# One written order per pass, with named PSUM tiles, for the three Fourier layers of a token-fusion kernel

## The chip, the cores and the metric
The kernel runs on one core of a Trainium2 chip. The metric is the device time of one execution in microseconds (us), lower is better; a profile of one execution gives the instructions of each engine with their times.

## The reference, cut to what matters
64 images of 256x256 go through a Fourier neural operator of four layers with 32 channels, then through one attention and feed-forward block together with 77 text rows. Per layer:
```python
x_ft = jnp.fft.rfft2(v)                        # only 24 x 12 modes are kept
out1 = jnp.einsum('bixy,ioxy->boxy', x_ft[:, :, :M1, :M2], W1)
out2 = jnp.einsum('bixy,ioxy->boxy', x_ft[:, :, -M1:, :M2], W2)
x1 = jnp.fft.irfft2(out_ft, s=(Sx, Sy))        # out_ft: zeros, with out1 and out2 set
x2 = jnp.einsum('bcxy,cd->bdxy', v, w_w[i]) + w_b[i][None, :, None, None]
v = x1 + x2
v = (v - mean) * jax.lax.rsqrt(var + BN_EPS)   # mean, var over batch, x, y
v = v * bn_g[i][None, :, None, None] + bn_b[i][None, :, None, None]
if i < L - 1:
    v = jax.nn.relu(v)
```

## The kernel before
The images lie in HBM as `v`, 1 MB for each of the 8 chunks of a batch element. Each of layers 0, 1 and 2 is one call of `layer(i, ...)`, which makes one pass per batch element `b` (64 passes). It turns the mixed modes of `mix_d[i]` into the layer's activated image, stores it, and at once takes the forward transforms of that image and the sums of squares for the next layer. The statements run under `tc.manual_schedule()`, so each engine executes its instructions in the order in which they are written. SP issues all loads and stores of the layer, in written order too.

The steps of a pass, with their lines:
- `load_am` (L574), `scale_am` (L594, on POOL): the modes of one batch element are loaded into a buffer `am` and multiplied by the batch-norm scale (spread out in `sk`) into one of two tiles `ams`.
- `spread` (L605, L609): the inverse transform along x. Two groups of matmuls fill PSUM, and VectorE (DVE) transposes each in 32x32 blocks, straight from PSUM, into `y_`.
- `pre(b, t)`, once for each chunk: inverse transform along y (L624) and, from layer 1 on, the 1x1 convolution of the loaded chunk `vin` (L635), into two PSUM tiles; relu into `vo`, one half by ScalarE (ACT, L642), one by DVE (L643); the store of `vo` (L644); a block transpose of `vo` into `t32` on DVE (L647). `load_v` (L588) then loads the chunk four ahead. In layer 0 there is no `vin`; the input rows come with `load_x`.
- `product(b, t)`: `vo` times the next layer's weights (L659), and on ACT the square with a running sum (L666), whose result goes back to PSUM.
- `along_y(b)`: the forward transform along y, 128 matmuls in a row over all of `t32` (L676), then two block transposes out of PSUM into `zt` on DVE (L686).
- `along_x(b)`: the forward transform along x (L699), an ACT copy (L706) and a store (L707).

All PSUM tiles come from one pool `lp` of four buffers, each two banks, named `ring` in the profile, taken in turn. `vo` comes from a pool `lo` of four buffers, `vin` from `li` of four, `t32` from `lt` of five. The order of a pass is that of two loops at the end of `layer`: for each chunk, `pre` of it and `product` of the one before; after chunk 1 `along_y`, and after chunk 3 `along_x`, of the batch element before; after chunk 5 `spread` of the next.

Of the kernel before, what the change touches and what calls it, by code (L numbers as in the profile page):

```python
# [16 lines left out]
S = 256  # L17
C = 32
# [107 lines left out]


# [8 lines left out]
def tile_fno_fusion_transformer(ctx: ExitStack, tc: tile.TileContext, a, cst_d, grid_d, out):  # L136
# [371 lines left out]
    def layer(i, st, src, dst, acc):  # L508
# [7 lines left out]
        with ExitStack() as cx:  # L516
            def pool(name, bufs, **kw):
# [3 lines left out]
            op, yp, ap_, cp, xp, zp, tp = (  # L521
                pool(n, k, reuse_waits="tile")
                for n, k in (("lo", 4), ("ly", 2), ("la", 2), ("lc", 1), ("lx", 2), ("lz", 1), ("lt", 5))
            )
            pp = pool("lp", 4, space=PSUM)
# [29 lines left out]
            sk = cp.tile([128, 16, 32], F32, name="sk")  # L555
            for _, p0, cs in halves:
                nc.vector.tensor_copy(
                    sk[p0:p0 + 64],
                    s_[p0:p0 + 64, cs].rearrange("p (c o) -> p c o", o=1).to_broadcast([64, 16, 32]),
                )  # L560
# [8 lines left out]
            am, y_, t32, vin, vo = {}, {}, {}, {}, {}  # L569

            def load_am(b):
                am[b] = ap_.tile([128, 16 * C], F32, name="am")
                for n in range(2):
                    nc.sync.dma_start(  # L574
                        am[b][64 * n:64 * n + 2 * KX],
                        mix_d[i][b].rearrange("p k c -> (p k) c")[:, 512 * n:512 * n + 512],
                    )
# [12 lines left out]
            def scale_am(b):  # L590
                a_ = am.pop(b)
                for n in range(2):
                    hv = slice(64 * n, 64 * n + 2 * KX)
                    nc.gpsimd.tensor_tensor(  # L594
                        ams[b % 2][hv], a_[hv], sk[hv].rearrange("p c k -> p (c k)"), ALU.mult
                    )

            def spread(b):

                y_[b] = yp.tile([128, 2, 32, C], F32, name="y_")  # L600
                for h in range(2):
                    ps = pp.tile([128, 2, 512], F32, name="ring")
                    for n in range(2):
                        hv = slice(64 * n, 64 * n + rows_)
                        nc.tensor.matmul(  # L605
                            ps[:, n, :], lhsT=EX[hv, 128 * h:128 * h + 128], rhs=ams[b % 2][hv],
                            start=True, stop=True, skip_group_check=True,
                        )
                    nc.vector.transpose(  # L609
                        y_[b][:, h].rearrange("p q c -> p c q"),  # L610
                        ps.rearrange("p n (c k) -> p (n c) k", k=32),
                    )

            def four():

                t2 = [pp.tile([128, 2, 512], F32, name="ring") for _ in range(2)]
                return t2, [t2[n // 2][:, n % 2] for n in range(4)]

            def pre(b, t):
                t2, ps = four()  # L620
# [9 lines left out]
                if i:  # L630
                    v = vin.pop((b, t))
                    for k in range(4):
                        for n in range(4):
                            j = (n + k) % 4
                            nc.tensor.matmul(  # L635
                                ps[n][32 * j:32 * j + 32], lhsT=ws[32 * n:32 * n + 32],
                                rhs=v[32 * n:32 * n + 32, 2 * j:2 * j + 2, :], start=False, stop=True,
                                skip_group_check=True, tile_position=(32 * n, 32 * j),
                            )
                o = vo[b, t] = op.tile([128, 8, S], F32, name="vo")  # L640
                of = o.rearrange("p (n r) y -> p n (r y)", r=2)
                nc.scalar.activation(of[:, 0:2], t2[0], AF.Relu)  # L642
                nc.vector.tensor_scalar(of[:, 2:4], t2[1], 0.0, None, ALU.max)  # L643
                nc.sync.dma_start(dst[b][:, t], o)  # L644
                if t % 2 == 0:
                    t32[b, t // 2] = tp.tile([128, 8, 16, C], F32, name="t32")
                nc.vector.transpose(  # L647
                    t32[b, t // 2][:, :, 8 * (t % 2):8 * (t % 2) + 8, :].rearrange("p y s c -> p s y c"),
                    o.rearrange("p s (y l) -> p s y l", l=32),
                )  # L650

            def product(b, t):

                o = vo.pop((b, t))
                t2, ps = four()
# [8 lines left out]
                for n in range(2):  # L664
                    at = 2 * (8 * b + t) + n
                    nc.scalar.activation(t2[n], t2[n], AF.Square, accum_out=acc[:, at:at + 1])  # L666

            zts = {}

            def along_y(b):  # L670
                t2, ps = four()
                for k in range(8):
# [9 lines left out]
                for j in range(4):  # L682
                    t32.pop((b, j))
                zt = zts[b] = zp.tile([128, 2, 32, C], F32, name="zt")
                for h in range(2):
                    nc.vector.transpose(  # L686
                        zt[:, h].rearrange("p k c -> p c k"),
                        t2[h].rearrange("p n (s c) -> p c (n s)", c=C),
                    )

            def along_x(b):
                zt = zts.pop(b)
                ps = pp.tile([128, 2, 512], F32, name="ring")
                for g in range(3):
                    n = 0
                    for h in range(2):
                        for r in range(2):
                            k0 = M * r + 4 * g
                            nc.tensor.matmul(  # L699
                                ps[:, 0, 96 * g:96 * g + 96],  # L700
                                lhsT=zt[:, h, k0:k0 + 4, :].rearrange("p k c -> p (k c)"),
                                rhs=FX[:, h, 48 * r:48 * r + 96], start=n == 0, stop=n == 3,
                            )
                            n += 1
# [4 lines left out]
            load_am(0)  # L709
# [5 lines left out]
            scale_am(0)  # L715
            spread(0)
            for b in range(B + 1):
                for t in range(8):
                    if b < B:
                        pre(b, t)  # L720
                        nb, nt = (b, t + 4) if t < 4 else (b + 1, t - 4)
                        if i and nb < B:
                            load_v(nb, nt)
                    pb, pt = (b, t - 1) if t else (b - 1, 7)
                    if pb >= 0 and (b < B or t == 0):
                        product(pb, pt)
                    if b and t == 1:
                        along_y(b - 1)
                    if b and t == 3:
                        along_x(b - 1)  # L730
                    if b + 1 < B:
                        if t == 0:
                            load_am(b + 1)
                            if i == 0:
                                load_x(b + 1)
                        if t == 2:
                            scale_am(b + 1)
                        if t == 5:
                            spread(b + 1)
# [408 lines left out]
```

## Time and profile before

| what | value |
|---|---|
| median of 3 runs (lowest, highest) | 12364.16 us (12347.56, 12374.95) |
| the profiled execution, its own time | 12360.58 us |
| its span in the profile | 12358.8 us, 405064 instructions |
| busy in the span: PE, PEld | 11164.5 us (90%), 5874.0 us (48%) |
| busy in the span: DVE, ACT, POOL | 8774.8 us (71%), 6094.5 us (49%), 1412.7 us (11%) |
| DMA | 3485.06 MB, mean 282 GB/s |
| relu of half a chunk: ACT L642, DVE L643 | 1021 ns, 1209 ns |
| transpose of a chunk, DVE L647 | 2311 ns |
| square of half a chunk, ACT L666 | 1012 ns, and 190 ns to read the sum |
| transpose out of PSUM, DVE L686 | 1925 ns |

PE is TensorE's matmul, PEld its weight load, which overlaps with matmuls; matmuls are pipelined, so their durations overlap too. A line such as "L643 DVE TENSOR_SCALAR vo<-ring" names the source line, the engine, the operation, and the tile written and read. In a timeline the first two numbers are the start and the duration in us; brackets give the idle time of the engine before it and what ended it, "issue" where the profile shows nothing that it waited for. SPq is SP's queue of DMA issues; the short times there are those of issuing, not of moving the data.

### The profile page before, as it was taken

What the parts mean: (1) busy time and instruction counts of PE and PEld (TensorE: products, weight loads), DVE (VectorE), ACT (ScalarE), POOL (GpSimd) and SP (SyncE); (2) the same over time, 40 slices, a digit from 0 to 9 for tenths busy, and PEclk for the clock granted to TensorE, in tenths of its full rate; (3) what the DMA queues carried; (4) which work ended last, traced back from release to release, by engine and by line L of the source; (5) the groups of instructions that cost most, each with busy time, mean ns of one, the idle gap of its engine ahead of it and who ended that gap; (6) DMA issues with size and microseconds to landing.
All of it is one profiled execution on the core that took longest, in us unless ns stands there. A gap on an engine that the chain in (4) does not pass through costs nothing. (4 is left out here: it accounts for less than half of the span.)

```text
span 12358.8 us, 405064 instructions
## 1 busy us (share of the span) xinstructions
PE 11164.5 (90%) x182038; PEld 5874.0 (48%) x182038; DVE 8774.8 (71%) x10667; ACT 6094.5 (49%) x10249; POOL 1412.7 (11%) x1987
## 2 busy tenths in 40 slices
PE   6999999998799999999979999999999699999999
PEld 3444444443444444444434444444444366666666
DVE  6777777777776777777766777767777566666665
ACT  5555555555555555555544555555555333333333
POOL 0000000000000000000010000000000133333333
PEclk8999999999899999999989999999999799999999
DMA  7555555555899999888889989889899755555554
GB/s 226 200 199 203 203 201 201 201 200 210 325 354 349 349 351 350 348 347 348 346 302 352 354 346 355 339 339 353 346 351 352 247 234 227 219 228 233 218 223 152
DMA packets 589283, 3485.06 MB, mean 282 GB/s; under 512 B 95000, under 2 KB 144536, under 8 KB 188568
## 3 DMA queue, kind: packets, MB, share of 16 engines
q1 hardware_dynamic: 539520, 3392.84, 71.2%
q0 software_dynamic: 40880, 62.59, 2.0%
q8 instruction: 1423, 23.31, 0.8%
q10 hardware_dynamic: 7144, 3.72, 0.1%
q14 instruction: 316, 2.59, 0.1%
HBM read 1761.87 MB, written 1696.92 MB: 280 GB/s over the span
## 5 line engine op out<-in xcount | busy, mean ns | idle before, releaser
L666 ACT ACTIVATE ring<-ring 128x1024 f32<-128x1024 f32 x3072 | 3108.8, 1012 | 1186.4 <-PE ring L659 1148.7
L647 DVE STREAM_TRANSPOSE t<-vo 128x2048 f32<-128x2048 f32 x1536 | 3550.0, 2311 | 175.1 <-ACT vo L642 14.5
L659 PE MATMUL ring<-vo,w 32*32 32x512 f32 x49152 | 2849.3, 622 | 392.2 <-DVE zt L686 138.7
L642 ACT ACTIVATE vo<-ring 128x1024 f32<-128x1024 f32 x1536 | 1568.2, 1021 | 2997.7 <-PE ring L635 2378.9
L643 DVE TENSOR_SCALAR vo<-ring 128x1024 f32<-128x1024 f32 x1536 | 1857.7, 1209 | 608.2 <-PE ring L635 420.4
L676 PE MATMUL ring<-t,cst 32*32 32x512 f32 x49152 | 1864.7, 601 | 303.7 <-issue 302.1
L686 DVE STREAM_TRANSPOSE zt<-ring 128x1024 f32<-128x1024 f32 x384 | 711.8, 1925 | 1658.6 <-PE ring L676 1658.6
L659 PEld LDWEIGHTS ring<-vo,w 32*32 32x32 f32 x49152 | 761.3, 105 | 1898.7 <-ACT ring L666 477.0
L676 PEld LDWEIGHTS ring<-t,cst 32*32 32x32 f32 x49152 | 975.9, 103 | 1157.0 <-issue 707.8
L594 POOL TENSOR_TENSOR ams<-am,sk 48x512 f32<-48x512 f32 x384 | 486.9, 1268 | 8642.4 <-DMA am<-mix 8039.9
L635 PE MATMUL ring<-vin,ws 32*32 32x512 f32 x32768 | 1238.0, 606 | 22.1 <-issue 19.8
L699 PEld LDWEIGHTS ring<-cst,zt 128*128 128x128 f32 x4608 | 536.4, 194 | 174.6 <-ACT vo L642 161.6
L666 ACT ACTIVATION_READ_ACCUMULATOR ring<-ring 128x1 f32 x3072 | 584.1, 190 | 0.0
L1097 POOL DMA_DIRECT2D out_dram<-o x1024 | 504.4, 501 | 659.8 <-DVE o L1092 628.2
L699 PE MATMUL ring<-cst,zt 128*128 128x96 f32 x4608 | 568.7, 281 | 8.1 <-DVE zt L686 8.1
L896 PE MATMUL hp<-ch,win 128*32 128x512 f32 x4096 | 472.0, 601 | 8.3 <-DMA ch<-v 8.1
L635 PEld LDWEIGHTS ring<-vin,ws 32*32 32x32 f32 x32768 | 253.5, 103 | 407.9 <-issue 377.8
L605 PE MATMUL ring<-ams,cst 49*128 49x512 f32 (+1 forms) x1536 | 391.5, 621 | 37.6 <-POOL ams L594 27.2
L901 ACT ACTIVATE h<-hp,hbias 128x512 f32<-128x512 f32 x64 | 44.0, 687 | 595.5 <-PE hp L896 595.5
L419 PE MATMUL mps<-wm,xh 32*64 32x128 f32 (+1 forms) x4608 | 121.3, 374 | 203.4 <-ACT e L431 74.1
L1059 PE MATMUL pp<-zs,w 128*128 128x165 f32 x2048 | 302.1, 305 | 0.0
L1070 PE MATMUL pp<-g,w 128*128 128x165 f32 x2048 | 298.6, 303 | 0.0
(936 smaller groups left out, 11812.8 us busy)
## 6 DMA issues: line engine op xcount, KB each, us to landing
v<-vo SPq DMA_DIRECT2D x1536, 1024.0 KB
vin<-v SPq DMA_DIRECT2D x1024, 1024.0 KB
ch<-v SPq DMA_DIRECT2D x512, 1024.0 KB
mix<-ob SPq DMA_DIRECT2D x96, 512.0 KB
am<-mix SPq DMA_DIRECT2D x384, 96.0 KB
xin<-in_x_dram SPq DMA_DIRECT2D x16, 1024.0 KB
mv<-in_x_dram SPq DMA_DIRECT2D x256, 64.0 KB
out_dram<-o POOLq DMA_DIRECT2D x1024, 16.0 KB, 3.0
```

The source lines that it names most:

```text
L594: nc.gpsimd.tensor_tensor(ams[b % 2][hv], a_[hv], sk[hv].rearrange("p c k -> p (c k)"), ALU.mult)
L635: nc.tensor.matmul(ps[n][32 * j:32 * j + 32], lhsT=ws[32 * n:32 * n + 32], rhs=v[32 * n:32 * n + 32, 2 * j:2 * j + 2, :], start=False, sto ...
L642: nc.scalar.activation(of[:, 0:2], t2[0], AF.Relu)
L643: nc.vector.tensor_scalar(of[:, 2:4], t2[1], 0.0, None, ALU.max)
L647: nc.vector.transpose(t32[b, t // 2][:, :, 8 * (t % 2):8 * (t % 2) + 8, :].rearrange("p y s c -> p s y c"), o.rearrange("p s (y l) -> p s ...
L659: nc.tensor.matmul(ps[n][32 * j:32 * j + 32], lhsT=w4[i + 1][32 * n:32 * n + 32], rhs=o[32 * n:32 * n + 32, 2 * j:2 * j + 2, :], start=Tru ...
L666: nc.scalar.activation(t2[n], t2[n], AF.Square, accum_out=acc[:, at:at + 1])
L676: nc.tensor.matmul(ps[n][32 * j:32 * j + 32], lhsT=FYT[32 * n:32 * n + 32, k, :], rhs=t32[b, j][32 * n:32 * n + 32, k].rearrange("p s c -> ...
L686: nc.vector.transpose(zt[:, h].rearrange("p k c -> p c k"), t2[h].rearrange("p n (s c) -> p c (n s)", c=C),)
L699: nc.tensor.matmul(ps[:, 0, 96 * g:96 * g + 96], lhsT=zt[:, h, k0:k0 + 4, :].rearrange("p k c -> p (k c)"), rhs=FX[:, h, 48 * r:48 * r + 9 ...
L896: nc.tensor.matmul(hp[32 * g:32 * g + 32], lhsT=win[:, 7 - t:39 - t], rhs=ch[:, g], start=False, stop=t == 7, skip_group_check=True,)
L1097: nc.gpsimd.dma_start(out[b, 64 * n + 16 * g:64 * n + 16 * g + 16].rearrange("(p t) d -> p t d", t=2), o[32 * g + 8 * n:32 * g + 8 * n + 8 ...
```

## The change
The loops at the end of `layer` are replaced by a list of named steps, one list for layer 0 (`_FIRST`) and one for layers 1 and 2 (`_LATER`). Each entry is a step, a mark for the batch element that it works on (`'` one before the pass's, `''` two before, `^` one after), and its arguments, divided by points. The steps are the old ones, taken apart:
- `F(b, t, slots, by)` is the matmuls of `pre`, followed by `load_v`; `D` its relu and store, with a letter for each half, `a` for ACT and otherwise DVE; `T` the transpose of the chunk.
- `U(b, t, slots)` is the matmuls of `product`, `S` its two squares (all on ACT in both lists).
- `Z(b, k0, 2, slots)` is a quarter of `along_y`; `W(b, h, by)` takes one half out of PSUM: `v` as before by a transpose, `a` by an ACT copy into SBUF (`zs0`, `zs1`), from which `w` transposes later.
- `X` is `along_x`. `Y(b, h, slot, by)` and `y` are one half of `spread`, with the same two ways.

PSUM is four named tiles, ringA to ringD, and each entry says which it takes. `load_am` loads straight into `ams`, two batch elements ahead, and `scale_am` multiplies in place; `am` and `sk` are gone. `load_x` is issued at the start of a pass. The pool `lo` has five buffers in layer 0 and four later. The loop runs two passes more than there are batch elements, where before it ran one more.

```diff
+_FIRST = """
+    S'6.aa T'7 S'5.aa F0.CA.ad D0 U'7.BD w''1 S'7.aa U'2.CA S'2.aa F1.DB.aa T0 D1 F4.AC.da Y^0.D.a T'2 D4
+    Y^1.B.a U1.AD S1.aa X''C T'3 T'5 U0.BD Z'0.2.AC S0.aa F3.DB.da Z'2.2.AC D3 U3.BD S3.aa Z'4.2.AC y^1 T1
+    U4.DB Z'6.2.AC T4 S4.aa y^0 W'1.a W'0.v F5.DB.ad D5 F6.AD.ad F7.BC.ad D6 D7 F2.AD.ad U6.CB D2 U5.AD T6
+""".split()
+_LATER = """
+    Y^0.D.a w''1 U'7.CA S'7.aa T'1 F0.BD.aa D0 Y^1.C.a F1.AB.da U'6.CD D1 U0.AB S'6.aa S0.aa X''C T'7
+    F2.CB.da U'5.DA D2 F3.CB.da S'5.aa Z'0.2.AD Z'2.2.AD D3 U2.BC S2.aa y^0 Z'4.2.AD U3.CB T2 Z'6.2.AD y^1
+    S3.aa W'1.a F5.DC.aa W'0.v D5 F4.BA.aa T3 D4 T0 F7.CD.ad D7 U1.AB T4 S1.aa U4.DC S4.aa T5 F6.BA.da D6 T6
+""".split()
...
-            op, yp, ap_, cp, xp, zp, tp = (
+            op, yp, cp, xp, zp, tp = (
                 pool(n, k, reuse_waits="tile")
-                for n, k in (("lo", 4), ("ly", 2), ("la", 2), ("lc", 1), ("lx", 2), ("lz", 1), ("lt", 5))
-            )
-            pp = pool("lp", 4, space=PSUM)
+                for n, k in (("lo", 5 if i == 0 else 4), ("ly", 2), ("lc", 1), ("lx", 2), ("lz", 1), ("lt", 5))
+            )
+            pp = pool("lp", 1, space=PSUM)
...
+            def slot(n):
+                return pp.tile([128, 2, 512], F32, name=f"ring{n}")
...
             def load_am(b):
-                am[b] = ap_.tile([128, 16 * C], F32, name="am")
                 for n in range(2):
                     nc.sync.dma_start(
-                        am[b][64 * n:64 * n + 2 * KX],
+                        ams[b % 2][64 * n:64 * n + 2 * KX],
...
             def scale_am(b):
-                a_ = am.pop(b)
+                for _, p0, cs in halves:
+                    v = ams[b % 2][p0:p0 + 2 * KX].rearrange("p (c k) -> p c k", k=32)
+                    s = s_[p0:p0 + 2 * KX, cs].rearrange("p (c o) -> p c o", o=1)
+                    nc.gpsimd.tensor_tensor(v, v, s.to_broadcast([2 * KX, 16, 32]), ALU.mult)
...
+            def D(b, t):
+                t2, by = fs.pop((b, t))
                 o = vo[b, t] = op.tile([128, 8, S], F32, name="vo")
                 of = o.rearrange("p (n r) y -> p n (r y)", r=2)
-                nc.scalar.activation(of[:, 0:2], t2[0], AF.Relu)
-                nc.vector.tensor_scalar(of[:, 2:4], t2[1], 0.0, None, ALU.max)
+                for n in range(2):
+                    if by[n] == "a":
+                        nc.scalar.activation(of[:, 2 * n:2 * n + 2], t2[n], AF.Relu)
+                    else:
+                        nc.vector.tensor_scalar(of[:, 2 * n:2 * n + 2], t2[n], 0.0, None, ALU.max)
                 nc.sync.dma_start(dst[b][:, t], o)
...
+            def W(b, h, by):
+                ps = zs[b][0][h].rearrange("p n k -> p (n k)")
+                if by == "a":
+                    ev["z", b, h] = zp.tile([128, 1024], F32, name=f"zs{h}")
+                    nc.scalar.copy(ev["z", b, h], ps)
+                else:
+                    ev["z", b, h] = ps
+                    w(b, h)
...
-            for b in range(B + 1):
-                for t in range(8):
-                    if b < B:
-                        pre(b, t)
...
-                    if b and t == 1:
-                        along_y(b - 1)
-                    if b and t == 3:
-                        along_x(b - 1)
...
-                        if t == 5:
-                            spread(b + 1)
...
+            for b in range(B + 2):
+                if i == 0 and b + 1 < B:
+                    load_x(b + 1)
+                if b + 2 < B:
+                    load_am(b + 2)
+                    scale_am(b + 2)
+                for f, at, args in order:
+                    if 0 <= b + at < B and (b or f is not Y or at):
+                        f(b + at, *args)
```

## The prediction
> **What bounds the kernel now.** I read the stages first, then one pass of each kind of layer in the order of time, then the DMA share inside it. The three stretches below are layers 0, 1 and 2 (first `spread` to last `along_x`); columns are the stretch, its length, busy time of PE, PEld, DVE, ACT, POOL, the granted clock, DMA share, GB/s.
> ```profile
> 189.00:3071.00 2882.00, 2614.17 (x43010) 1217.22 (x43010) 2222.41 (x1286) 1602.51 (x2625) 168.44 (x139) 0.95 0.54 201
> 3175.00:6371.00 3196.00, 2918.05 (x59680) 1385.73 (x59676) 2271.16 (x1297) 1646.01 (x2637) 181.06 (x164) 0.99 0.90 347
> 6445.00:9608.00 3163.00, 2913.03 (x59369) 1379.81 (x59338) 2258.99 (x1280) 1636.35 (x2624) 164.81 (x137) 0.99 0.90 347
> ```
> They are 9241 of 12358.8 us. PE's busy time overlaps itself; no compute engine is full. Layers 1 and 2 differ from layer 0 in the DMA column: 0.90 against 0.54.
>
> Layer 0, one pass (timeline):
> ```profile
> 2026.45 2.31 DVE L647 STREAM_TRANSPOSE t<-vo 128x2048 f32<-128x2048 f32 x1
> 2028.69 1.19 DVE L643 TENSOR_SCALAR vo<-ring 128x1024 f32<-128x1024 f32 x1
> 2029.98 2.31 DVE L647 STREAM_TRANSPOSE t<-vo 128x2048 f32<-128x2048 f32 x1
> ...
> 2029.98 8.81 PE L676 MATMUL ring<-t,cst 32*32 32x512 f32 x256
> ...
> 2038.79 3.67 DVE L686 STREAM_TRANSPOSE zt<-ring 128x1024 f32<-128x1024 f32 x2 [6.50 <-PE ring L676]
> 2039.89 1.02 ACT L642 ACTIVATE vo<-ring 128x1024 f32<-128x1024 f32 x1 [7.37 <-PE ring L624]
> 2040.77 0.14 PEld L659 LDWEIGHTS ring<-vo,w 32*32 32x32 f32 x4 [1.32 <-DVE zt L686]
> ```
> See two regimes. In the chunk loop DVE has no pause: 1.29 + 2.24 = 3.53 us a chunk. Then `along_y` holds PE for 8.8 us while DVE (6.50) and ACT (7.37) wait, and afterwards PE waits for DVE's two block transposes out of PSUM. A transpose of `t` at 2008.24 recurs at 2052.51: a pass takes 44.27 us.
>
> Layer 1, the end of a pass in four stretches, columns as above:
> ```profile
> 4650.00:4654.00 4.00, 4.00 (x100) 2.22 (x89) 0.00 (x0) 0.00 (x0) 1.26 (x1) 0.68 0.99 403
> 4654.00:4658.00 4.00, 4.00 (x75) 1.46 (x52) 3.32 (x2) 0.76 (x1) 1.28 (x2) 1.00 0.21 82
> 4658.00:4660.00 2.00, 1.58 (x37) 0.67 (x40) 1.90 (x3) 0.48 (x2) 0.00 (x0) 1.00 0.00 0
> 4660.00:4664.00 4.00, 4.00 (x88) 2.06 (x81) 3.81 (x3) 3.64 (x6) 0.00 (x0) 1.00 0.93 299
> ```
> The same pass in the timeline of SP's queue and POOL:
> ```profile
> 4639.48 1.92 SPq L574 DMA_DIRECT2D am<-mix  x2
> 4642.57 0.43 SPq L588 DMA_DIRECT2D vin<-v  x1
> ...
> 4652.74 2.62 POOL L594 TENSOR_TENSOR ams<-am,sk 48x512 f32<-48x512 f32 x2 [45.59 <-DMA am<-mix]
> ...
> 4659.54 0.32 SPq L644 DMA_DIRECT2D v<-vo  x1
> ```
> The 96 KB `am` loads, issued at 4639.5 to 4641.4, are usable only at 4652.7: they stood behind the stores and loads before them. DMA runs without a break until about 4654.6, is idle about 5 us because nothing was issued between 4643.0 and 4659.5, and restarts. 258 chunks in 1600 us give 6.20 us a chunk, 49.6 us a pass; 0.894 of that (SP's queue 88.5% and instructions 0.9%) is 44.3 us of DMA work. So in these layers a better compute order can't beat 44 us.
>
> [...] here a 16 KB `out_dram` store lands after 3.0 us, which I use. [...]
>
> **The change part by part.**
> 1. PE's work per pass is the same: 8 F (`pre`), 8 U (`product`), `along_y` in four pieces Z, X, Y. Zero.
> 2. ACT gets three 128x1024 copies out of PSUM (two Y, one W; 1.0 us by the row of L642), and relu halves move: 9 on ACT and 7 on DVE in layer 0, 11 and 5 later, where it was 8 and 8. ACT per pass: 16 squares x 1.03 (start to start) + 9 x 1.0 + 3.3 = 28.8 us; later 30.8. Below any bound: no cost by itself.
> 3. Three of four y/z transposes now read SBUF. Not shown before: between 1.2 us (half of `t`) and 1.9 (strided, as now); I take 1.75, the present start to start, since the strided result stays. DVE in layer 0: 8 x 2.24 + 7 x 1.24 + 4 x 1.75 = 33.6 us (31.9 with the low value).
> 4. POOL multiplies in place with a broadcast operand in place of `sk`; `am` is loaded two batches ahead, so its 1.27 us pieces have a whole pass to hide in. `load_x` leads by a pass. Their SP entries move ahead of the pass's stores, and wait on readers that are done. Zero; if wrong, at most one 1.3 us piece a pass.
> 5. Order. I walked one pass by hand with times of the trace: F to its relu 1.18 us (layer 0) or 2.3 (later, two groups), U to its square 1.35, a square frees its slot after 1.1 and the second after 2.15, a relu after 1.05 (ACT) or 1.25 (DVE), a two-k piece of Z 1.8, X 2.9, Y 1.0.
> **Layer 0**: ACT's squares S'6, S'5 end at 4.2; F0, D0 5.65; S'7 and S'2 9.85; D1, both Y copies and D4's half 15.1; S1 17.25; U0, S0 21.05; F3, D3 23.5; U3, S3 27.5; U4, S4 31.1; F5, D5 33.4; F6, F7, F2 follow at 33.5, 34.6, 36.0; D2 38.4; the next S'6 38.6. DVE is busy 33.6 of it. Against 44.27: -5.8 us x 64 = **-371 us**. Bounds: DVE full, 34.5 (-625); three late hand-offs of 1.2 us, 42 (-145). The fifth `vo` buffer keeps stores away: DMA needs 0.54 x 44.27 = 24 us.
> **Layers 1 and 2**: the slots alone give about 43.8 us, PE's own work under 40. But `vo` keeps 4 buffers, and U and T of chunks are put off, so a buffer is held longer. The instruction order shows D6 waiting for the store of chunk 4, two chunks back, and the next pass's D1 for the store of chunk 6, 6.7 us after it is issued. Before, D waited for the store four chunks back (14.8 us). Now count DMA from the load after F5, where the queue starts empty: load, S5, load, S4, load, S7, load, S6, eight transfers of 1 MB at 403 GB/s = 2.6 us, and 3.0 us fixed: store 6 lands at **23.8**. D1 starts there; queued behind it on ACT are S'6 and S0, on DVE T'7 and D2, and PE's U0 waits for its slots. From D1 to the next F5's end: S'6 frees X's slot 2.15, X and its copy 5.9, F2, D2 9.6, F3, D3 13.3, Z'0 and Z'2 15.3, U2, S2 18.9, U3, S3 22.3, W' copy 23.4, F5 **25.5**. Sum 49.3 us, against 49.6: -0.3 x 128 = **-38 us**. What is late next is the DMA restart: idle 5 us a pass, as now. Bounds: 44.5 (store wait absent) and 52 (below).
> 6. Fill: one more partial pass per layer, setup of `sk` gone: within 30 us, taken as 0.
>
> Sum against the profiled execution (12360.6 us, 1.8 outside its 12358.8 us span): -409, 11952; the median of the runs is 3.6 above that execution, so **11955**.
>
> **Rivals.**
> - *The store wait doesn't bind* (transfers land sooner, or D1's chain is shorter than my walk). Then slots and DMA bind near 45.5: -371 - 4.1 x 128 = -896, 11468. For: the slot walk is 43.8, the DMA work 44.3. Against: the 13 us queue seen by `am`.
> - *Slower: PE starves in layers 1 and 2.* PE's weight loads of L676 waited 314.7 us for "issue" in layer 1, 4.9 a pass, while DMA was full, and the clock fell to 0.68 at 4650. If such gaps come on top of the D1 chain, with PE cold after the waits for stores, 53.2 us a pass: +3.6 x 128 - 371 = +90, 12454. It decides from 49.6 + 371/128 = 52.5 us a pass. Against: Z is cut in pieces, so instruction bursts are shorter.
> - *The order isn't what runs.* The layers stand under a manual schedule and the built queues follow the list; otherwise about 12364.
>
> **How the numbers follow.** Main case (48 to 51 us later) 0.55, its own range 11750 to 12200; no store wait 0.30; slower 0.11; nothing changed 0.04. A measurement of this kernel tells 0.2%, 25 us, from no change. Faster 0.85, same 0.04, slower 0.11. The range 11380 to 12340 leaves out the best end of the second case and most of the third.
>
> **What would show it.** Right: layer 0 about 2510 us with DVE near 0.87 and no DVE wait of 6 us on Z; in layers 1 and 2 about 49 us a pass, ACT and DVE at D1 and D6 (and the PE behind them) waiting for DMA of `v<-vo`, DMA idle before F5. Wrong: DMA share of 0.95 or more there (second case), or "issue" waits above 6 us a pass (third). A layer 0 above 42 us a pass breaks the first step.

## The result, and the profile after

The changed kernel takes 13397.85 us (median of 4 runs, 13390.38 to 13414.53) where the kernel before took 12369.56 beside it: ratio 1.0836, 95% interval 1.0816 to 1.0855. It is slower by 8.4%; the forecast was 11955 with a range up to 12340. The profiled execution took 13390.38 us, its span is 13388.6.

The stretches of layers 0, 1 and 2 (length, busy time of PE, PEld, DVE, ACT, POOL, granted clock, DMA share, GB/s):
```profile
197.00:3063.00 2866.00, 2305.78 (x42998) 1256.65 (x42998) 2134.85 (x1217) 1839.79 (x2878) 135.48 (x136) 0.91 0.56 202
3162.00:6843.00 3681.00, 3001.84 (x59394) 1358.04 (x59394) 2006.83 (x1092) 1976.57 (x3006) 138.95 (x139) 0.91 0.80 299
6945.00:10637.00 3692.00, 3006.51 (x59394) 1355.10 (x59394) 2007.36 (x1093) 1976.58 (x3006) 138.97 (x139) 0.91 0.79 299
```
Layer 0 is nearly as long as before (2866 us against 2882), where a gain of 371 us was forecast. Layers 1 and 2 are each some 500 us longer, and their DMA share fell from 0.90 to 0.80. Share times length is about the same as before (2945 and 2876 us in layer 1), so the extra time is pauses of DMA. The clock fell from 0.99 to 0.91.

Waits in the middle of layer 1 (4000 to 6000 us, 35 passes; total, times, longest):
```profile
PEld ringA L690 <- ACT vo L670: 208.7, 71, 6.4
ACT vo L670 <- DMA v<-vo: 193.8, 37, 6.7
DVE vo L672 <- DMA v<-vo: 178.5, 35, 6.3
DVE vo L672 <- PE ringD L690: 173.3, 35, 7.3
```
L670 and L672 are the relu halves of D on ACT and DVE, L654 and L643 the matmuls of F, L690 those of U, L701 the squares S, L716 Z, L678 T, L632 the transposes of y, L735 those of the y transform. Once a pass both relu engines wait some 5 us for a store, and PE waits behind ACT; once a pass (35 times) they also wait for a U. The places, in the timelines of ACT and of DVE:
```profile
5039.28 1.02 ACT L670 ACTIVATE vo<-ringA 128x1024 f32<-128x1024 f32 x1 [4.92 <-DMA v<-vo]
...
5047.14 1.02 ACT L670 ACTIVATE vo<-ringB 128x1024 f32<-128x1024 f32 x1 [2.45 <-PE ringD L654]
...
5051.76 1.02 ACT L670 ACTIVATE vo<-ringB 128x1024 f32<-128x1024 f32 x1 [1.78 <-PE ringD L690]
```
```profile
5039.30 1.23 DVE L672 TENSOR_SCALAR vo<-ringB 128x1024 f32<-128x1024 f32 x1 [4.59 <-DMA v<-vo]
5040.63 2.31 DVE L678 STREAM_TRANSPOSE t<-vo 128x2048 f32<-128x2048 f32 x1
5042.86 2.02 DVE L735 STREAM_TRANSPOSE zt<-zs 128x1024 f32<-128x1024 f32 x1
5044.75 2.31 DVE L678 STREAM_TRANSPOSE t<-vo 128x2048 f32<-128x2048 f32 x1
```
The first line of each is D6, waiting for the store of chunk 4. The second ACT line is D0 of the next batch element: it starts as DVE's fourth operation, T'1, ends. The third is D1. It takes the buffer of chunk 6, and what it waits for is not that chunk's store but U'6 (L690), the last step on PE that reads it: in the passes between 4000 and 6000 us D1 starts 0.07 us (median) after the last matmul of U'6. Stretches of this pass, columns as above:
```profile
5016.00:5019.00 3.00, 1.27 (x44) 0.65 (x46) 0.00 (x0) 0.00 (x0) 0.00 (x0) 1.00 0.14 52
5019.00:5022.00 3.00, 2.17 (x55) 0.93 (x51) 0.85 (x1) 2.90 (x5) 0.00 (x0) 1.00 0.00 0
...
5037.00:5040.00 3.00, 0.00 (x0) 0.00 (x0) 0.70 (x1) 0.72 (x1) 0.00 (x0) 0.68 1.02 431
5040.00:5043.00 3.00, 2.65 (x36) 0.91 (x40) 2.90 (x3) 1.66 (x3) 0.00 (x0) 0.50 1.00 423
```
DMA is idle ahead of F5's load (5024.70), then full; while it is full, D6 waits, PE stands still, and after that its clock is 0.50.

Layer 0, DVE's timeline at the end of the y transform:
```profile
2000.11 2.31 DVE L678 STREAM_TRANSPOSE t<-vo 128x2048 f32<-128x2048 f32 x1 [3.67 <-PE ringC L716]
2002.35 1.87 DVE L632 STREAM_TRANSPOSE y__19803<-zs 128x1024 f32<-128x1024 f32 x1
2004.06 1.86 DVE L735 STREAM_TRANSPOSE zt<-ringA 128x1024 f32<-128x1024 f32 x1
2005.77 1.20 DVE L672 TENSOR_SCALAR vo<-ringB 128x1024 f32<-128x1024 f32 x1
```
T4 waits until Z'6 has read `t32`, and y^0 and W'0 stand behind it. F6 needs the slot that W'0 empties.

**Where the 1030 us went**, from the stores of `xo` in SP's queue, one for each batch element: the 63 intervals from the first to the last in each layer, and the rest. The last interval or two of a layer are short, since little is left to do there (18.9 us for the last one in layer 0 after the change); the median interval of layer 0 is 44.3 us, and was 44.6.

| part | predicted, us | measured, us |
|---|---|---|
| layer 0, 63 passes (44.65 to 43.86 us each) | -371 | -50 |
| layers 1 and 2, 126 passes (49.1 to 56.35) | -38 | +910 |
| fill, drain and the way between layers | 0 | +170 |
| sum | -409 | +1030 |

### The profile page after: what moved, and what is told of

Its sections match the earlier page's. It is cut to its first block, busy times and chain, and to the rows that moved or that the text cites. A ratio compares the mean times of both kernels' runs of the same rounds, so it can differ in the third digit from the quotient of the medians.

```text
span 13388.6 us, 404421 instructions
## 1 busy us (share of the span) xinstructions
PE 11039.6 (82%) x182038; PEld 5864.0 (44%) x182038; DVE 8176.2 (61%) x10213; ACT 7012.8 (52%) x11267; POOL 1326.4 (10%) x1987
## 3 DMA queue, kind: packets, MB, share of 16 engines
q8 instruction: 1425, 23.35, 0.7%
## 5 line engine op out<-in xcount | busy, mean ns | idle before, releaser
L678 DVE STREAM_TRANSPOSE t<-vo 128x2048 f32<-128x2048 f32 x1536 | 3480.8, 2290 | 253.5 <-PE ringC L716 221.3
L716 PE MATMUL ringA<-t,cst 32*32 32x512 f32 x24576 | 2082.5, 603 | 72.2 <-issue 66.8
L690 PE MATMUL ringA<-vo,w 32*32 32x512 f32 x11264 | 989.7, 688 | 707.4 <-ACT vo L670 526.5
L716 PE MATMUL ringD<-t,cst 32*32 32x512 f32 x16384 | 1416.1, 606 | 76.8 <-issue 76.2
L670 ACT ACTIVATE vo<-ringB 128x1024 f32<-128x1024 f32 x832 | 851.3, 1023 | 1152.5 <-PE ringB L654 379.6
L690 PE MATMUL ringC<-vo,w 32*32 32x512 f32 x12288 | 1377.3, 673 | 65.2 <-issue 31.3
L701 ACT ACTIVATE ringB<-ringB 128x1024 f32<-128x1024 f32 x832 | 842.0, 1012 | 966.0 <-PE ringC L690 533.7
L690 PE MATMUL ringB<-vo,w 32*32 32x512 f32 x13312 | 1261.9, 635 | 38.1 <-issue 31.8
L716 PEld LDWEIGHTS ringA<-t,cst 32*32 32x32 f32 x24576 | 804.0, 103 | 641.8 <-issue 414.9
L701 ACT ACTIVATE ringC<-ringC 128x1024 f32<-128x1024 f32 x768 | 777.3, 1012 | 548.0 <-PE ringB L690 319.5
L690 PE MATMUL ringD<-vo,w 32*32 32x512 f32 x12288 | 992.3, 636 | 45.9 <-DVE vo L672 33.1
L654 PE MATMUL ringB<-vin,ws 32*32 32x512 f32 x12288 | 980.5, 675 | 0.0
L672 DVE TENSOR_SCALAR vo<-ringC 128x1024 f32<-128x1024 f32 x320 | 392.0, 1225 | 938.0 <-PE ringB L654 913.8
L670 ACT ACTIVATE vo<-ringA 128x1024 f32<-128x1024 f32 x384 | 392.3, 1022 | 1049.1 <-DMA v<-vo 674.3
L735 DVE STREAM_TRANSPOSE zt<-ringA 128x1024 f32<-128x1024 f32 x192 | 366.2, 1907 | 869.3 <-PE ringA L716 555.7
L701 ACT ACTIVATE ringD<-ringD 128x1024 f32<-128x1024 f32 x768 | 778.9, 1014 | 99.9 <-PE ringB L690 88.4
L672 DVE TENSOR_SCALAR vo<-ringD 128x1024 f32<-128x1024 f32 x320 | 391.5, 1223 | 657.1 <-PE ringB L643 320.5
L672 DVE TENSOR_SCALAR vo<-ringA 128x1024 f32<-128x1024 f32 x256 | 313.5, 1225 | 707.0 <-PE ringD L690 644.0
L690 PEld LDWEIGHTS ringA<-vo,w 32*32 32x32 f32 x11264 | 230.2, 110 | 1152.2 <-ACT vo L670 784.9
L701 ACT ACTIVATE ringA<-ringA 128x1024 f32<-128x1024 f32 x704 | 714.9, 1016 | 24.0 <-PE ringB L690 5.3
L672 DVE TENSOR_SCALAR vo<-ringB 128x1024 f32<-128x1024 f32 x192 | 233.4, 1216 | 640.5 <-DMA v<-vo 637.4
```

The lines of the kernel that those rows point to most:

```text
L654: nc.tensor.matmul(ps[n][32 * j:32 * j + 32], lhsT=ws[32 * n:32 * n + 32], rhs=v[32 * n:32 * n + 32, 2 * j:2 * j + 2, :], start=False, sto ...
L670: nc.scalar.activation(of[:, 2 * n:2 * n + 2], t2[n], AF.Relu)
L672: nc.vector.tensor_scalar(of[:, 2 * n:2 * n + 2], t2[n], 0.0, None, ALU.max)
L678: nc.vector.transpose(t32[b, t // 2][:, :, 8 * (t % 2):8 * (t % 2) + 8, :].rearrange("p y s c -> p s y c"), vo[b, t].rearrange("p s (y l) ...
L690: nc.tensor.matmul(ps[n][32 * j:32 * j + 32], lhsT=w4[i + 1][32 * n:32 * n + 32], rhs=o[32 * n:32 * n + 32, 2 * j:2 * j + 2, :], start=Tru ...
L701: nc.scalar.activation(q, q, AF.Square, accum_out=acc[:, at:at + 1])
```

## The experiments

Pass lengths in us by the same count, and medians:

| kernel | layer 0 | layer 1 | layer 2 | median |
|---|---|---|---|---|
| before | 44.65 | 49.07 | 49.19 | 12369.6 |
| after | 43.86 | 56.34 | 56.36 | 13397.9 |
| e1_old_order | 44.89 | 48.18 | 48.23 | 12282.9 |
| e2_five_vo | 43.87 | 47.82 | 47.68 | 12276.6 |
| e3_filler | 43.92 | 56.83 | 56.87 | 13485.4 |
| e4_w_first | 44.07 | 56.57 | 56.78 | 13448.6 |
| e5_swap_t1 | 43.86 | 55.64 | 55.72 | 13308.0 |
| e6_t1_in_pass | 43.87 | 56.52 | 56.16 | 13400.7 |
| e7_y0_ahead | 41.17 | 56.73 | 56.56 | 13247.3 |
| e8_filler_full | 43.87 | 58.08 | 58.26 | 13632.2 |
| e9_five_y0 | 41.48 | 47.93 | 47.56 | 12129.2 |
| e10_new_lists | 41.01 | 47.26 | 47.49 | 12044.0 |
| e11_direct | 50.52 | 53.46 | 53.23 | 13464.9 |
| e12_old_load_after | 44.87 | 49.23 | 49.08 | 12408.1 |
| e13_swap_filler | 43.86 | 54.59 | 54.64 | 13180.9 |
| e14_more_traffic | 44.91 | 56.30 | 56.64 | 13504.7 |

For layer 1, the moments at which SP issues a pass's transfers, counted from F5's load; means over the passes between 4000 and 6000 us whose issues the timeline lists singly (these passes are 0.4 to 0.9 us longer than the mean above, which includes the short intervals at the end of a layer):

| kernel | store 6 | store 0 | store 1 | `xo` | store 3 | next F5 load |
|---|---|---|---|---|---|---|
| after | 16.4 | 24.9 | 29.2 | 33.6 | 41.0 | 57.0 |
| e2_five_vo | 11.7 | 17.4 | 20.3 | 24.5 | 31.8 | 48.6 |
| e3_filler | 16.3 | 25.0 | 29.6 | 34.0 | 41.4 | 57.7 |
| e5_swap_t1 | 16.4 | 23.9 | 28.4 | 32.7 | 40.0 | 56.3 |
| e6_t1_in_pass | 13.4 | 17.8 | 26.4 | 33.3 | 41.0 | 57.3 |
| e8_filler_full | 16.3 | 24.9 | 31.0 | 35.5 | 42.8 | 58.7 |
| e13_swap_filler | 16.3 | 22.9 | 27.3 | 31.6 | 38.9 | 55.0 |

**e1_old_order: the old order in the new code.**
```diff
+_OLD = """
+    F0.AB.ad D0 T0 U'7.CD S'7.aa F1.AB.ad D1 T1 U0.CD S0.aa Z'0.8.AB W'0.v W'1.v
+    F2.CD.ad D2 T2 U1.AB S1.aa F3.CD.ad D3 T3 U2.AB S2.aa X'C F4.DA.ad D4 T4 U3.BC S3.aa
+    F5.DA.ad D5 T5 U4.BC S4.aa Y^0.D.v Y^1.A.v F6.BC.ad D6 T6 U5.DA S5.aa F7.BC.ad D7 T7 U6.DA S6.aa
+""".split()
+_FIRST = _LATER = _OLD
```


> The steps, the named PSUM tiles, the early load of the modes and the in-place scaling of the change are kept; only the list is replaced: one list for all three layers that writes out the order of the kernel before (each chunk transposed at once, both halves of y and of the y transform taken out by DVE, the tiles' names turned by one a pass so that they follow the old ring, four vo buffers everywhere). Theory (the new order is what costs): within 60 us of the kernel before, about 12370 us, layer 0 near 2880 us and layers 1 and 2 near 3190 us each. Rival (naming of the tiles, in-place scaling on POOL, or the load that now precedes the store in SP's queue costs): above 12600 us, layers 1 and 2 above 3350 us.

Measured: 12282.87 us, ratio to before 0.9929 (0.9906 to 0.9951). With the order of the kernel before the whole loss is gone. The new code around it is even somewhat faster than the old, more than either theory had; e12 takes that up.

**e2_five_vo: one more `vo` buffer in layers 1 and 2.**
```diff
-                for n, k in (("lo", 5 if i == 0 else 4), ...
+                for n, k in (("lo", 5), ...
```


> A fifth vo buffer in layers 1 and 2 as well, nothing else. Theory (the wait for the store at D6 and the cold TensorE after it make layers 1 and 2 slow): the waits of ACT and DVE for DMA of v<-vo go below 1 us a pass, PE keeps its clock, a pass falls from 56 to between 46 and 50 us, layers 1 and 2 from 3685 to about 3100 us each, the whole to about 12250 us. Rival (the waits are a symptom: the compute chain of the new order, with transposes from SBUF and copies, is itself over 53 us): a pass of 53 us or more, the whole above 13000 us. Layer 0 stays at 2866 us.

Measured: 12276.58 us, 1121 less than the changed kernel; ratio to before 0.993 (0.9908 to 0.9953). Between 4000 and 6000 us DVE no longer waits for `v<-vo`, and ACT only 14.2 us in 41 passes, and the stretch has its clock and its DMA share back:
```profile
4000.00:6000.00 2000.00, 1782.50 (x38287) 839.16 (x38277) 1291.15 (x700) 1274.89 (x1934) 85.66 (x82) 0.98 0.89 354
```
By the table of issues a pass is 8.4 us shorter in the middle of the layer: 4.7 of it up to store 6 (D6's own wait) and 4.2 between stores 6 and 1, while the way from store 1 to the next F5 (27.8 and 28.3) is the same with and without store waits. So the loss comes from the new order with only four buffers: the old order with four (e1) does not have it, and the new order with five does not either. A fifth buffer under the old order was not tried. In all, the new order with five buffers (12276.6) is no faster than the old one with four (12282.9): its passes are 1.0 us shorter in layer 0 and about 0.5 in the others, but fill and drain are 115 us longer. The next runs ask what the 4.2 are.

**e3_filler: matmuls that keep PE busy while D6 waits.** In layers 1 and 2, `K.10.D` stands ahead of `Y^0.D.a`:
```diff
+            def K_(b, n, n_):
+                ps = slot(n_)
+                for q in range(n):
+                    nc.tensor.matmul(ps[:, q % 2, 0:256], lhsT=EX[0:K, 0:128], rhs=T4[0:K, :], ...)
```


> In layers 1 and 2, ten matmuls of 128x256 into the tile of ringD, whose result nobody reads, stand ahead of the y transform at the start of each list pass, where PE waits for the store; everything else is as in the changed kernel, and the store wait stays. Theory (half of the loss is TensorE's clock, which falls to 0.5 after the idle stretch): the clock stays near 1 in the stretch after D6, the pass falls from 56 to about 50 to 52 us, 500 to 700 us less in all, about 12800 us. Rival (the wait itself is the whole loss, the clock hides behind it): no gain, 13300 to 13500 us, as PE has ten matmuls more to do.

Measured: 13485.44 us, no gain; store 0 and store 1 come as late as in the changed kernel. The clock as half of the loss, the theory here, is not borne out; but the filler was not a full test: in the three microseconds after D6 the clock was still 0.69 (stretch of this run):
```profile
5082.00:5085.00 3.00, 2.90 (x36) 0.68 (x36) 2.89 (x2) 1.99 (x2) 0.00 (x0) 0.69 1.03 434
```

**e4_w_first: layer 0, W' ahead of T4 and y^0.**
```diff
-    ... Z'6.2.AC T4 S4.aa y^0 W'1.a W'0.v F5.DB.ad ...
+    ... Z'6.2.AC S4.aa W'1.a W'0.v T4 y^0 F5.DB.ad ...
```


> Only the list of layer 0 is changed: the two takings of the y transform (W'1 by a copy, W'0 by a transpose out of PSUM) stand ahead of T4 and y^0 instead of behind them. Theory (F6 waits 4.6 us a pass for W'0 behind these two on DVE, and PE is cold after that): a pass of layer 0 falls from 44.1 to 36 to 40 us, layer 0 from 2866 to 2350 to 2600 us, the whole to 12900 to 13130 us. Rival (DVE or the slots bind elsewhere, the wait moves to the next step): less than 1.5 us a pass, the whole above 13300 us. Layers 1 and 2 stay.

Measured: 13448.64 us; layer 0 does not gain (44.07 us a pass). The wait moved. PE's waits from 700 to 2700 us, first of the changed kernel, then of this run:
```profile
PE ringA L643 <- DVE zt L735: 206.5, 45, 4.8
```
```profile
PE ringB L643 <- DVE vo L672: 163.0, 45, 3.7
```
F6 hardly waits for W'0 any more, but F7, which writes ringB next, now waits until D5's half on DVE has emptied it, since that is queued behind T4 and y^0.

**e5_swap_t1: T'1 ahead of w''1 on DVE.**
```diff
-    Y^0.D.a w''1 U'7.CA S'7.aa T'1 F0.BD.aa D0 ...
+    Y^0.D.a T'1 w''1 U'7.CA S'7.aa F0.BD.aa D0 ...
```


> Four vo buffers as in the changed kernel; in the list of layers 1 and 2 only two steps on DVE change places: T of chunk 1 of the batch element before now comes ahead of the transpose w of the y transform. Theory (the second half of the loss is that D0 takes the buffer of chunk 1, which its transpose frees, and that this transpose is fourth on DVE behind D6, T6 and w): D0 starts 1.9 us earlier in every pass, which cuts a pass from 56 to about 54, 200 to 260 us in all; the wait at D6 stays near 5 us. Rival (the stretch after D6 is long because TensorE is cold): no change beyond 30 us, since nothing on PE is moved.

Measured: 13308.04 us, 90 less. Store 0 comes 1.0 us earlier, not 1.9, and D6's wait is unchanged. The direction is the theory's; half of the size or more is not there (200 to 260 us were expected).

**e6_t1_in_pass: T1 ahead of D6.**
```diff
-    Y^0.D.a w''1 U'7.CA S'7.aa T'1 F0.BD.aa D0 ... F7.CD.ad D7 U1.AB T4 ...
+    Y^0.D.a w''1 U'7.CA S'7.aa F0.BD.aa D0 ... F7.CD.ad D7 T1 U1.AB T4 ...
```


> Four vo buffers; T of chunk 1 is moved out of the next pass to the place ahead of T4, so that chunk 1 gives its buffer up before D6. Theory (which store a D waits for is set by where the list frees buffers): the waits of 5 us at D6 and the late D0 both go; what is late next is D1, which then waits for the store of chunk 6, the wait that the prediction had; the pass falls to about 52 to 53 us, the whole to 12900 to 13050. Rival (four buffers and the load traffic make a store wait of 5 us anywhere, so moving it gains nothing): above 13300. Rival (without D6's wait the chain is free): below 12500, as with five buffers.

Measured: 13400.69 us, the same as the changed kernel. Store 6 and store 0 come 3.0 and 7.1 us earlier. At D1, which now waits for the store of chunk 6, 4.3 of the 7.1 are lost, and the rest by `xo` (ACT's timeline, and a stretch behind it):
```profile
5061.32 1.02 ACT L670 ACTIVATE vo<-ringB 128x1024 f32<-128x1024 f32 x1 [6.88 <-DMA v<-vo]
```
```profile
5064.00:5067.00 3.00, 3.00 (x27) 2.41 (x12) 0.81 (x1) 2.54 (x6) 0.00 (x0) 0.50 1.01 426
```
From store 1 to `xo` takes 6.9 us here and 4.4 in the changed kernel: X runs at the clock of 0.50. The first rival was right: with four buffers the store wait moves and nothing is gained.

**e7_y0_ahead: layer 0, y^0 ahead and T4 behind D6.**
```diff
-    ... Z'4.2.AC y^1 T1 U4.DB Z'6.2.AC T4 S4.aa y^0 W'1.a W'0.v F5.DB.ad D5 F6.AD.ad F7.BC.ad D6 D7 ...
+    ... Z'4.2.AC y^0 y^1 T1 U4.DB Z'6.2.AC S4.aa W'1.a W'0.v F5.DB.ad D5 F6.AD.ad F7.BC.ad D6 T4 D7 ...
```


> Only the list of layer 0 is changed: y^0 goes to the place of y^1, where DVE is idle for some 4 us, the takings of the y transform stand ahead of the rest, and T4 goes behind D6. So DVE has only W'0, D5 and D6 to do between the end of Z'6 and the next need of PE. Theory (in layer 0 DVE's order after Z'6 is one link of the loop, and moving only W'0 put the other transposes ahead of D5 and D6): a pass falls from 43.6 to about 42, some 100 us in all. Rival (the slots bind by themselves, DVE has no part): within 30 us of the changed kernel.

Measured: 13247.25 us, 151 less; a pass of layer 0 falls by 2.7 us to 41.17, more than expected. DVE's written order after Z'6 is a link of the loop.

**e8_filler_full: the filler on all 128 rows.**
```diff
-                        ps[:, q % 2, 0:256], lhsT=EX[0:K, 0:128], rhs=T4[0:K, :],
+                        ps[:, q % 2, 0:256], lhsT=ONES, rhs=FYT.rearrange("p k m -> p (k m)"),
```


> The filler once more, with eight matmuls that use all 128 rows (ones by a table, 128x256), in place of ten on 24 rows, since after those the clock still fell to 0.7 behind D6. Theory, as it stands after that run (the clock is not on the path: D0 waits for a buffer, not for PE): the clock is above 0.9 in the 9 us after D6 and the pass still takes 55 to 57 us. Rival (cold clock): a pass of 52 us or less, 500 us less in all.

Measured: 13632.18 us; the pass is 58.2 us, above the range given. The stretches after D6, then DVE's and ACT's timelines:
```profile
5046.00:5049.00 3.00, 3.00 (x52) 1.19 (x52) 3.00 (x2) 2.14 (x4) 0.00 (x0) 1.00 1.01 423
5049.00:5052.00 3.00, 0.84 (x6) 0.30 (x4) 2.59 (x2) 0.33 (x1) 0.00 (x0) 0.96 1.02 411
5052.00:5055.00 3.00, 2.25 (x28) 1.44 (x44) 0.00 (x0) 2.51 (x3) 0.83 (x1) 0.50 0.98 373
```
```profile
5049.30 2.29 DVE L678 STREAM_TRANSPOSE t<-vo 128x2048 f32<-128x2048 f32 x1
```
```profile
5051.67 1.02 ACT L670 ACTIVATE vo<-ringB 128x1024 f32<-128x1024 f32 x1 [3.36 <-issue]
```
With the clock at 1.00, F0 is done 2.4 us earlier than in the changed kernel (its load is issued at 19.6 in place of 22.0), but D0 starts only 0.08 us after T'1 ends, at 51.59, and store 0 is as late as before. In that new pause PE turns cold, and F1 and U'6 run at 0.50.

**e13_swap_filler: the edits of e5 and e8 together.**

> Four vo buffers; the swap of T'1 and w from the fifth experiment and the full-row filler from the eighth together. Theory (D0's buffer and the clock cover for each other: with only one removed the other holds the same stretch): D0 starts about 2 us earlier and PE has no pause over 3 us between D6 and D1, so the stretch from the store of chunk 6 to that of chunk 1 falls from 12.8 to 9 to 10.5 us and the pass to 53 to 54.5, 12950 to 13100 us in all. Rival (the store of chunk 6 or something else sets D1 anyway): a stretch of 12 us or more, 13250 us or more in all.

Measured: 13180.93 us, 217 less than the changed kernel, where e5 alone gave 90 and e8 lost 234. From store 6 to store 1 it takes 11.0 us: between the two theories, 1.8 less than in the changed kernel and 2.4 more than with five buffers. So the two do cover for each other. The traces place the last 2.4 us (medians between 4000 and 6000 us): D0 starts 4.7 us after store 6, with five buffers 3.7; and D1 starts 1.4 us after F1's last matmul, again as U'6 ends, where with five buffers, not needing the buffer of chunk 6, it starts 0.2 us after.

**e14_more_traffic: more DMA traffic in layer 0.**
```diff
                 nc.sync.dma_start(dst[b][:, t], o)
+                if i == 0 and t % 2 == 0:
+                    nc.sync.dma_start(src[b][:, t], o)
```


> The changed kernel, and in layer 0 the even chunks are stored twice, the second time to the image buffer that is free in this layer (it is overwritten in layer 1), so DMA moves 12 MB a pass there instead of 8; layers 1 and 2 are unchanged. Theory (PE's idle time marked issue grows with DMA traffic[...]): the idle time marked issue ahead of the weight loads of Z in layer 0 rises from 2.5 us a pass to 4 to 6, layer 0 from 43.6 to 46 to 48 us a pass. Rival (that idle time belongs to the instruction mix): it stays at 2 to 3 us a pass, and the pass at 43.6 to 46 us, of which up to 2 from the longer hold of the vo buffers.

Measured: a pass of layer 0 takes 44.91 us, 1.0 more; 13504.69 in all. The idle time ahead of Z's weight loads (L716, L718 here) from 700 to 2700 us, of the changed kernel (45 passes) and of this run (44), and of e2 from 4000 to 6000 us in layer 1 (41 passes):
```profile
  issue: 114.8, 410
```
```profile
  issue: 139.8, 410
```
```profile
  issue: 170.1, 270
```
That is 2.6, 3.2 and 4.1 us a pass, with DMA shares of 0.56, 0.75 and 0.89. The kernel before had 5.0 us a pass in layer 1 (203.3 us in 41 passes, L676), with a share of 0.90. So it rises with the traffic, here by less than the theory's range (4 to 6), and the pass stays in the rival's range; layer 1 differs from layer 0 in its instruction mix too.

**e9_five_y0: e2 and e7 together.**

> The fifth vo buffer of the second experiment and the layer-0 list of the seventh together. Theory (they work in different layers and add): 12277 less about 150, 12100 to 12150 us. Rival (one of the two gains came from something that both share, such as the clock or the fill between layers): above 12200.

Measured: 12129.16 us, ratio to before 0.9812 (0.9792 to 0.9831). They add.

**e10_new_lists: five buffers and two new lists.**
```diff
+    S'6.aa F0.CA.da S'5.aa T'7 D0 T'2 U'7.BD U'2.CA T0 S'7.aa S'2.aa F1.DB.ad D1 F4.AC.da Y^0.D.a D4 Y^1.B.a
+    U1.AD w''1 S1.aa T'5 T'3 X''C U0.BD Z'0.2.AC F3.DB.da S0.aa D3 Z'2.2.AC U3.BD Z'4.2.AC Z'6.2.AC T1 y^1
+    W'0.v U4.DB S3.aa F5.CD.da T4 W'1.a F6.AD.da S4.aa D5 D6 F7.CB.da F2.AD.aa U6.CB D7 T6 y^0 U5.AD D2
...
+    Y^0.D.a w''1 T'1 U'7.CA S'7.aa F0.BD.aa D0 Y^1.C.a F1.AB.da U'6.DC U0.BA D1 S'6.aa T'7 S0.aa X''D
+    F2.CB.ad U'5.AD D2 F3.CB.ad Z'0.2.AD U2.CB T2 S'5.aa D3 Z'2.2.AD y^1 Z'4.2.AD y^0 U3.BC T3 S2.aa Z'6.2.AD
+    F5.DC.ad S3.aa W'0.v W'1.a T0 F4.AB.ad D5 D4 F7.DC.ad D7 T4 U1.AB S1.aa U4.CD F6.AB.ad T5 S4.aa D6 T6
```


> Five vo buffers and both lists written anew, by walking the queues with the durations of the trace: in layers 1 and 2, U2 stands between Z'0 and Z'2 and F5 between Z'6 and the takings, so that loads and stores go out more evenly, and DVE takes more of the relu halves, so that ACT's squares come sooner; in layer 0 Z'6 comes ahead of the chunk's product, W'0 right behind it, and y^0 goes to the end. Theory (slots and the in-order queues bind, DMA has 44.3 us of work): a pass of about 45 us in layers 1 and 2 (e2 47.7) and 40 to 41 in layer 0, 11680 to 11850 us in all. Rival (with the fifth buffer the bound is DMA with its pauses or PE's instruction supply, which no list moves): within 80 us of the run with both simple edits, 12050 to 12200.

Measured: 12044.04 us, ratio to before 0.9736 (0.9720 to 0.9752), the fastest kernel here. Layer 0 came as expected. In layers 1 and 2 a pass takes about 47.4 us, not 45, so the whole is far above the theory's range and 6 us below the rival's. One thing the walk leaves out is PE's idle time marked issue: ahead of Z's weight loads it is 4.7 us a pass (197.6 us in 42 passes, from 4000 to 6000 us). That this is the rival's instruction supply was not shown.

**e11_direct: no ACT copies.**
```diff
-    Y^0.D.a w''1 ... Y^1.C.a ... y^0 ... y^1 ... W'1.a ...
+    Y^0.D.v ... Y^1.C.v ... W'1.v ...
```


> Five vo buffers and the changed kernel's lists, but y and the y transform are taken out of PSUM by DVE's transposes throughout (three ACT copies and three later transposes a pass become three transposes out of PSUM at the place of the copies). Theory (the copies are worth having because a slot comes free after 1.0 us on ACT instead of after DVE's queue and 1.9 us): 3 to 4 us a pass slower in layers 1 and 2 and about 4 to 5 in layer 0, 650 to 800 us more than with the copies, about 13000 us. Rival (the copies only add an instruction, since the transpose takes 1.9 us from either source): within 100 us of 12277.

Measured: 13464.92 us, 1188 more than e2 with the same buffers, and more than either theory: +6.6 us a pass in layer 0, +5.6 in layers 1 and 2. So the copies are worth far more than the instruction that each adds. That this is because a slot comes free earlier is the theory, not shown apart.

**e12_old_load_after: e1 with the load behind the store.**
```diff
+                nb, nt = (b, t + 4) if t < 4 else (b + 1, t - 4)
+                if i and nb < B:
+                    load_v(nb, nt)
```
These lines move from the end of `F` to behind the store in `D`.

> The first experiment (order of the kernel before in the changed code, 12283 us) with one edit: load_v is issued behind the chunk's store, as in the kernel before, instead of ahead of it. Theory (the 80 us by which that run beat the kernel before come from loads entering SP's queue before the store that waits for the relu): back to 12340 to 12390 us. Rival (they come from the modes being loaded two batch elements ahead and scaled in place): it stays at 12270 to 12300.

Measured: 12408.09 us, ratio to before 1.0036 (1.0021 to 1.0051). That is 18 us above the theory's range and far from the rival's. The load ahead of the store was worth 125 us; the rest of the new code costs about 47.

## Why the prediction was wrong

**Step 1 (PE's work the same)** held. The size of one of its parts did not: step 5 put a two-k piece of Z at 1.8 us, 7.2 for all four. The kernel before already shows more. The prediction's own line of L676 in layer 0 has 8.81 us for all 256 matmuls, 2.2 a piece, and in layer 1 all 256 take 12.5 us (median from 4000 to 6000 us), 3.1 a piece; one pass of layer 1 of the kernel before, in PE's timeline:
```profile
4641.54 5.20 PE L676 MATMUL ring<-t,cst 32*32 32x512 f32 x134
...
4648.77 5.91 PE L676 MATMUL ring<-t,cst 32*32 32x512 f32 x122 [2.04 <-issue]
```
In the changed kernel's layer 1 the four pieces take 2.4, 2.7, 3.3 and 3.2 us (medians from 4000 to 6000 us, each to the end of its last matmul). From store 3 to F5's load, where all four lie, the walk had 12.2 us (13.3 to 25.5); it takes 16.0 in the changed kernel and 16.8 with five buffers, where 4.1 us is idle time marked issue ahead of Z's weight loads. The walk from D1 to D3 before that was right: 13.3 against 12.8 (store 1 at 20.3, less 1.3 for its relu, to store 3 at 31.8). So the chain D1 to F5 was 4 us short, and the "slots alone 43.8" with it: e2 shows 47.7. The rival without a store wait, 45.5 us a pass, was too low for the same reason.

**Step 2 (ACT's copies cost nothing)** held, and missed what they are worth: with five buffers the same order without them is 1188 us slower (e11).

**Step 3** was close. Start to start, as the 1.75 was counted, the transposes from SBUF in layer 0 take 1.78 us (`y_`) and 1.98 (`zt`), medians from 700 to 2700 us, and `zt` out of PSUM 1.71. For the three from SBUF that is 0.3 us a pass more on DVE.

**Step 4 (loads moved, zero)** missed that `load_v` moved ahead of the chunk's store: that alone is a gain of 125 us in the old order (e12).

**Step 5, layer 0** failed in the way that the prediction named ("above 42 us a pass"). The walk let F6, F7 and F2 follow at 33.5 without looking at what W'0 is queued behind on DVE: T4, which waits for Z'6 because `t32` has five buffers, and y^0. F6 waited 4.6 us a pass for it. e4 shows that the wait goes on to D5's half on DVE, and by it to F7, if these two are only put behind W'0; e7 shows 2.7 us of it as a gain. The rest of the missing 5.4 us (43.86 against 44.27 less 5.8) fits the longer pieces of Z, 10.4 us for all four (medians from 700 to 2700 us, each to the end of its last matmul) against 7.2, but no run separates them in layer 0.

**Step 5, layers 1 and 2** is where the sign went. The mechanism was named: `vo` runs out, D6 waits for the store of chunk 4, DMA starts anew at F5. Store 6 was to land at 23.8 us after F5's load; in e6, where this store is what D1 waits for, D1 starts at 25.1 (store 1 at 26.4 less 1.3). So the price of that wait was nearly right. But the sum took it as the last wait before D1, and in the changed kernel it is not: D1 starts at 27.9, when U'6 has read the buffer. From store 6 to D1 the prediction had 6.7 us; it takes 7.3 with five buffers and 11.5 in the changed kernel. What lies between are waits that the sum put at nothing: D0 needs the buffer that T'1 frees, and T'1 is queued on DVE behind D6, T6 and w''1; and PE, idle for some 4 us while D6 waits, comes back at half its clock (0.50 from 5038.05 to 5048.29 in the pass shown). Moving T'1 ahead gains 90 us alone (e5), a warm PE alone (0.99 in the 3 us after store 6) gains nothing (e8 is 234 slower), and both gain 217 (e13). 27.9 and 29.1 for the chain from D1 to F5, which is longer by Z's pieces (step 1), make 57.0, against 23.8 and 25.5. The upper bound of 52 left no room for two terms that are off the same way.

**Step 6 (fill, within 30 us)** failed: it is 170 us. X works two batch elements behind its pass where it was one, so each layer fills and drains for longer: the first `xo` store comes at 299.0 us in place of 256.2, and between the last of a layer and the first of the next lie 231 and 243 us in place of 174. With five buffers 139 us of it are left; the old order in the new code (e1) has 24.

**The rivals.** The order did run. The slower case was right in its sign and in "cold after the waits for stores", wrong in what it put first: idle time marked issue ahead of Z's weight loads did not rise above 6 us a pass but fell, from 5.0 to 3.5 us (layer 1, 4000 to 6000 us), and what starts the loss is the buffer, as e2 shows. It was given 0.11 and 53.2 us, and 56.35 were measured.

## What to carry to other kernels

When steps that read a buffer are put off, count for every buffer the release of its last reader and its store, and put all of those waits into the sum; here three followed one another (D6, D0, D1), and the one that was priced did not come last. Take the time of a step from a pass of the same layer: a piece of Z at 1.8 us was short of what the trace of the kernel before already had. An engine's written order is part of a chain: moving one urgent step ahead helps only if what it overtook is not urgent for the next (in e4 it was: 44.07 us a pass, and 43.86 without the move). Before spending effort on an order, try one buffer more: here, under the new order, it was 8 KB a partition against 1121 us.

## What the runs showed of the hardware

The clock: in the trace of the changed kernel, the granted clock is 1.00 or 0.50, and from 3500 to 6200 us its 55 stretches at 0.50 last 3.41, 6.83, 10.24, 13.65 or 20.48 us, all multiples of 3.41. Stretches of that length around D6's wait in the pass shown (columns as above):
```profile
5034.64:5038.05 3.41, 1.98 (x8) 0.31 (x8) 0.06 (x1) 0.00 (x0) 0.00 (x0) 1.00 0.99 416
5038.05:5041.46 3.41, 1.11 (x28) 0.28 (x28) 2.06 (x2) 1.93 (x2) 0.00 (x0) 0.50 1.01 428
5041.46:5044.88 3.42, 3.42 (x52) 1.51 (x48) 3.42 (x3) 2.14 (x4) 0.00 (x0) 0.50 1.01 424
5044.88:5048.29 3.41, 3.41 (x39) 0.52 (x7) 2.17 (x2) 1.15 (x2) 0.00 (x0) 0.50 0.98 356
```
The clock falls to 0.50 after a stretch in which PE still had 1.98 us of matmuls. After the third, in which the profile shows PE without a pause, it does not return; it does after the fourth, at 5048.29, 7.9 us after PE restarted at 5040.35. With the fillers, too, matmuls without a pause did not always keep the clock up. In the 3 us after store 6 the mean clock is 0.51 in the changed kernel, 0.52 behind the ten matmuls on 24 rows, which fill 4.6 us without a pause (e3), and 0.99 behind the eight on 128 rows (e8; means over 34 or 35 passes from 4000 to 6000 us). The fillers differ in more than their rows, so what made this difference was not shown.

Idle time marked issue: the changed kernel's page has a DMA queue of the kind instruction that moved 23.35 MB, and PE's idle time marked issue ahead of Z's weight loads was larger where the DMA share was: 2.6 us a pass at 0.56 and 3.2 at 0.75 in the same layer (e14), 4.1 at 0.89 in layer 1 (e2). Whether PE waits there for its instructions was not shown.
